# The last three steps of two attentions in another order

## The chip, the cores and the metric

The kernel runs on one core of a Trainium2 chip. The metric is the device time of one execution in microseconds; lower is better. The engines are TensorE (PE: matmuls and transposes; PEld: its weight loads), VectorE (DVE), ScalarE (ACT), GpSimd (POOL) and the queues that issue transfers (SP among them).

## The reference, cut to what matters

A block in four stages over 16 batches of 100 tokens with 512 channels, all float32: a gated cross-attention with 16 heads, a mixture of 8 experts (top two, capacity 1024), a gated cross-attention with 8 heads, and a feed-forward stage with quantized weights. Both attentions look at the same context, 722 tokens of 384 channels per batch.

```python
def attention(x, context):                    # heads = 16 (first), 8 (second)
    q = (x @ Wq).reshape(B, Nq, heads, D).transpose(0, 2, 1, 3)
    k = (context @ Wk).reshape(B, Nkv, heads, D).transpose(0, 2, 1, 3)
    v = (context @ Wv).reshape(B, Nkv, heads, D).transpose(0, 2, 1, 3)
    attn = softmax(einsum('bhqd,bhkd->bhqk', q, k) * D**-0.5)
    return einsum('bhqk,bhkd->bqhd', attn, v).reshape(B, Nq, 512) @ Wo + bo

x = x + tanh(g_xattn[0]) * attention_0(layernorm(x), ctx)   # with biases bq, bk, bv
x = x + tanh(g_ffn[0])   * experts(layernorm(x))
x = x + tanh(g_xattn[1]) * attention_1(layernorm(x), ctx)
x = x + tanh(g_ffn[1])   * quantized_ffn(layernorm(x))
```

## The kernel before

The 1600 tokens lie as 13 tiles of 128 rows (the last has 64) in one buffer `x` on the chip through all four stages. Nothing of a stage is split off: the end of one runs into the start of the next, and the order in which PE gets its work is the order of the program's text (`manual_schedule(engines={PE})`). The order on DVE, ACT, POOL and the queues is made by the compiler's scheduler, with its own costs.

An attention runs in 64 steps, `steps = [(b, m) ...]`: batch b = 0 to 15, and within it four groups m of 128 channels. A group holds G heads, G = 4 in the first attention and 2 in the second. Step i does, in this order on PE:

- `peaks` (L399, tile `ps_mx`): transposes the running maxima `mx` of step i; DVE reduces them (L405).
- `scores(i+1, 0)` (L372, `ps_s`): the next step's scores for five of the six context chunks. ACT copies them to `raw_a` (L386), DVE takes the maxima over chunks (L389, twice).
- `softmax(i)` (L413, `ps_top`): PE spreads the maxima, DVE subtracts them (L421) into `pT`, ACT takes the exponential (L427), and POOL (G = 4) or DVE (G = 2) adds up the chunks (L430, `sm`). For the last batch with m > 0 these additions are left out, and PE sums all chunks itself.
- `scores(i+1, 1)`: the sixth chunk; ACT copies it (L382), DVE takes it into `mx` (L384).
- `attend(i-1)` (L442 and L453, `ps_pv`): the weighted sum over values and the sum of weights for the step before; DVE takes the reciprocal and multiplies (L461, L462) into `tT`.

Between these PE gets units of other work: `keys` (L216) and `values` (L241) of coming batches, `queries`, the input of queries, and `project` (L468, `ps_y`), which multiplies a finished tile by Wo; DVE adds it to `x` (L475). In the first attention each projection brings `moments` (L109, L110) and, in groups, `norm_scales` (L117 to L119), `normal` (L124), `turn` (L139) and `logits` (L657) of the router. `run` gives the units out: `extra[i]` holds those with a fixed step; keys and values lie in `todo` with a first and a last step, and are taken when they are due or while the step's cost is under an even share of what remains up to step 62. `cut` gives units of up to a cost of 2000 to the place between scores and softmax (`u[0]`), the others to the end of the step (`u[1]`).

Buffers that bear on the order: `pT` has two (`p2`), the banks of `ps_m` four, `raw_a` two, `mx` one. After the first attention come the last three tiles' router work (`norm_scales(LATE, NTT)`, `turn`, `logits`, filled up with the second attention's keys), and then the experts. After the second attention come the feed-forward stage's transposes (`ps_hT`, L1058). Its weights, their loads (L1011 to L1015) and the normalization of its first four tiles (L124, L1037, L109, L1046) start while the attention's last steps run, as soon as their memory comes free; projections 11 and 12 of the second attention are tied to come after the first dequantization (L1020) on DVE. G = 4 and G = 2 differ in one more thing: with G = 4 the softmax comes before the second scores and the sum, with G = 2 after them.

Of the kernel before, what the change touches and what calls it, by code (L numbers as in the profile page):

```python
# [17 lines left out]
B, T, C = 16, 100, 512  # L18
# [5 lines left out]
KC = C // P  # L24
# [39 lines left out]
def tiles_for(b):  # L64

    return [i for i in range(NTT) if (i * P + rows_of(i) - 1) // T == b]
# [76 lines left out]
class Attention:  # L143
# [352 lines left out]
    def run(self, done=(), after_project=None, more=()):  # L496

        steps = [(b, m) for b in range(B) for m in range(KC)]  # L500
        last_tile = lambda g: ((g + 1) * GT - 1) // P
        extra = {i: [] for i in range(-1, len(steps) + 40)}
        for at, *unit in more:
            extra[at].append(tuple(unit))
        for g in range(1, B // GB):
            at = 4 * KC * (g - 1)
            for n, i in enumerate(range(last_tile(g - 1) + 1, last_tile(g) + 1)):
                extra[at + 3 + n].append((self.query_input, i))
            for m in range(KC):
                extra[at + 7 + 2 * m].append((self.queries, g, m))  # L510
        for b in range(B):
            for i in tiles_for(b):

                at = (b + 1) * KC + (1 if b != B - 2 else KC - 1)
                extra[at].append((self.project, i))
                for later, *unit in after_project(i) if after_project else ():
                    extra[at + later].append(tuple(unit))
        todo = [u for b in range(1, B) for u in self.keys_and_values(b) if u not in done]

        def do(units):  # L520
            for f, *a in units:
                f(*a)

        def first(unit):

            f, b, n = unit[:3]
            return 4 * (b - 1) + n - 1 if f == self.keys else 4 * (b - 1) if b > 1 else -1

        def last(unit):

            f, b, n = unit[:3]
            return 4 * b + n - 2 if f == self.keys else 4 * b

        end = len(steps) - 2
        for i in range(-1, len(steps)):
            b, m = steps[max(i, 0)]
            if i >= 0 and m == 2 and b + 2 < B and b + 2 not in self.cxs:
                self.load_ctx(b + 2)

            whole = sum(map(self.cost, todo + sum((extra[j] for j in range(i, end)), [])))  # L540
            share = whole / max(1, end - i)
            units = list(extra[i])
            spent = sum(map(self.cost, units))
            for unit in sorted((u for u in todo if first(u) <= i), key=last):
                if last(unit) <= i or spent + self.cost(unit) / 2 <= share:
                    units.append(unit)
                    todo.remove(unit)
                    spent += self.cost(unit)

            units.sort(key=lambda u: u[0] in (self.keys, self.values) and first(u) == i)  # L550
            nxt = steps[i + 1] if i + 1 < len(steps) else None
            u = self.cut(units, 2000)
            if i >= 0:
                self.peaks(b, m)
            if nxt:
                self.scores(*nxt, 0)
            if self.G == 4:
                do(u[0])
                if i >= 0:
                    self.softmax(b, m)  # L560
            if nxt:
                self.scores(*nxt, 1)
            if i > 0:
                self.attend(*steps[i - 1])
            if self.G == 2:
                do(u[0])
                if i >= 0:
                    self.softmax(b, m)
            do(u[1])
        self.attend(*steps[-1])  # L570
        for i in range(len(steps), len(steps) + 40):
            do(extra[i])
# [1045 lines left out]
```

## Time and profile before

| what | us |
|---|---|
| median of 3 runs | 2733.43 (2732.81 to 2734.15) |
| the profiled execution: its time, its span | 2731.8, 2730.1 |
| PE busy, share of the span | 2682.5, 98% |
| first attention, to its last projection's end | 0 to 894 |
| experts | 894 to about 1590 |
| second attention, to its first closing projection | to 2354.5 |
| feed-forward stage | to 2730 |
| DVE busy in 853.6 to 886.7 and in 2324.2 to 2354.6 | 22.3 of 33.1, 20.7 of 30.4 |
| PE busy in the same two stretches | 25.2 of 33.1, 22.0 of 30.4 |

A line of a timeline gives the start, the duration, the engine, the line of the kernel, the operation, what it writes and reads, how many instructions were merged, and in brackets how long the engine stood idle before it and whose end released it. PEclk is the clock granted to TensorE, 1.00 at full speed. Matmul ends are modelled; the distance from one start to the next is the safer measure.

### The profile page before, as it was taken

What the parts mean: (1) busy time and instruction counts of PE and PEld (TensorE: products, weight loads), DVE (VectorE), ACT (ScalarE), POOL (GpSimd) and SP (SyncE); (2) the same over time, 40 slices, a digit from 0 to 9 for tenths busy, and PEclk for the clock granted to TensorE, in tenths of its full rate; (3) what the DMA queues carried; (4) which work ended last, traced back from release to release, by engine and by line L of the source; (5) the groups of instructions that cost most, each with busy time, mean ns of one, the idle gap of its engine ahead of it and who ended that gap; (6) DMA issues with size and microseconds to landing.
All of it is one profiled execution on the core that took longest, in us unless ns stands there. A gap on an engine that the chain in (4) does not pass through costs nothing. (4 is left out here: it accounts for less than half of the span.)

```text
span 2730.1 us, 45777 instructions
## 1 busy us (share of the span) xinstructions
PE 2682.5 (98%) x19716; PEld 1740.7 (64%) x19716; DVE 1201.2 (44%) x2010; ACT 859.0 (31%) x1194; POOL 499.3 (18%) x497
## 2 busy tenths in 40 slices
PE   8999999999998999999999999999999999899999
PEld 5666666666565688888888766666666566445554
DVE  4666676666667301010101077666565555611100
ACT  2545554545454100000000046333333333311110
POOL 2534444444442000000000042000000000301000
PEclk9999999999999899999999999999999999999999
DMA  5001000010001499989899432000000010610000
GB/s 167 18 18 34 18 29 22 18 45 18 18 29 57 169 360 348 320 313 321 310 318 319 166 91 63 21 22 29 17 23 27 17 34 1 185 62 16 12 12 10
DMA packets 129190, 278.33 MB, mean 102 GB/s; under 512 B 5825, under 2 KB 5841, under 8 KB 128465
## 3 DMA queue, kind: packets, MB, share of 16 engines
q1 hardware_dynamic: 117888, 246.80, 26.2%
q0 software_dynamic: 5968, 19.17, 2.1%
q10 hardware_dynamic: 5120, 9.31, 0.9%
q8 instruction: 160, 2.62, 0.4%
q14 instruction: 54, 0.43, 0.0%
HBM read 260.31 MB, written 14.94 MB: 101 GB/s over the span
## 5 line engine op out<-in xcount | busy, mean ns | idle before, releaser
L241 PE MATMUL ps_v<-wv_a,ctx_a 128*128 128x512 f32 (+1 forms) x1152 | 520.2, 599 | 1.0 <-DVE pT L421 0.5
L216 PE MATMUL ps_k<-ctx_a,wk_a 128*128 128x361 f32 x1488 | 485.5, 473 | 3.2 <-DVE pT L421 2.1
L874 PE MATMUL ps_h<-xT,w 128*128 128x128 f32 x3712 | 422.1, 276 | 4.0 <-DVEq L1503 4.0
L874 PEld LDWEIGHTS ps_h<-xT,w 128*128 128x128 f32 x3712 | 419.5, 193 | 4.7 <-issue 4.7
L216 PEld LDWEIGHTS ps_k<-ctx_a,wk_a 128*128 128x128 f32 x1488 | 272.6, 190 | 164.0 <-issue 18.3
L241 PEld LDWEIGHTS ps_v<-wv_a,ctx_a 128*128 128x128 f32 (+1 forms) x1152 | 204.8, 184 | 243.1 <-issue 229.9
L427 ACT ACTIVATE pT<-pT 128x1200 f32<-128x1200 f32 (+1 forms) x256 | 243.2, 953 | 258.2 <-DVE pT L421 248.0
L421 DVE TENSOR_TENSOR pT<-raw_a,ps_top 128x400 f32<-128x400 f32 (+4 forms) x384 | 279.0, 771 | 11.2 <-PE ps_top L413 11.0
L430 POOL TENSOR_TENSOR sm<-pT,sm 128x400 f32<-128x400 f32 x244 | 252.5, 1035 | 38.4 <-ACT pT L427 21.7
L389 DVE TENSOR_REDUCE raw_a<-raw_a 128x400 f32<-128x1200 f32 (+1 forms) x128 | 152.1, 1188 | 218.0 <-ACT raw_a L386 217.9
L386 ACT COPY raw_a<-ps_s 128x2000 f32<-128x2000 f32 (+1 forms) x128 | 180.3, 1408 | 154.1 <-PE ps_s L372 153.7
L372 PE MATMUL ps_s<-qT_a,kT_a 32*128 32x100 f32 (+3 forms) x4608 | 214.2, 277 | 3.4 <-ACT raw_a L386 1.2
L885 DVE TENSOR_TENSOR midT<-silu,ps_h 128x512 f32<-128x512 f32 x58 | 39.9, 688 | 390.4 <-PE ps_h L874 390.4
L894 PE MATMUL ps_o<-w,midT 128*128 128x512 f32 x464 | 203.9, 592 | 0.0
L372 PEld LDWEIGHTS ps_s<-qT_a,kT_a 32*128 32x128 f32 (+3 forms) x4608 | 180.1, 180 | 35.8 <-issue 22.7
L1100 PE MATMUL ps_z<-ffn_w,y_ffn 128*128 128x512 f32 (+1 forms) x416 | 190.8, 594 | 0.0
L248 ACT COPY v_a<-ps_v 128x512 f32<-128x512 f32 x192 | 111.3, 581 | 248.3 <-PE ps_v L241 248.3
L1082 PE MATMUL ps_y<-hT,ffn_w 128*128 128x384 f32 (+2 forms) x512 | 183.6, 503 | 0.0
L442 PE MATMUL ps_pv<-pT,v_a 128*32 128x100 f32 (+3 forms) x4608 | 163.2, 254 | 7.3 <-ACT pT L427 7.3
L442 PEld LDWEIGHTS ps_pv<-pT,v_a 128*32 128x32 f32 (+3 forms) x4608 | 135.5, 120 | 22.6 <-ACT pT L427 8.7
L1082 PEld LDWEIGHTS ps_y<-hT,ffn_w 128*128 128x128 f32 x512 | 95.1, 190 | 84.6 <-issue 50.3
L894 PEld LDWEIGHTS ps_o<-w,midT 128*128 128x128 f32 x464 | 85.9, 190 | 97.1 <-issue 97.1
(169 smaller groups left out, 2211.3 us busy)
## 6 DMA issues: line engine op xcount, KB each, us to landing
w<-in_L_ffn_w SPq DMA_DIRECT2D x116, 1024.0 KB
w<-in_L_ffn_wo SPq DMA_DIRECT2D x29, 2048.0 KB
ctx_a<-in_ctxT SPq DMA_DIRECT2D x30, 1083.0 KB
q<-in_L_ffn_fc_q SPq DMA_DIRECT2D x8, 1024.0 KB
ffn_w<-in_L_ffn_fc_scales SPq DMA_DIRECT2D x8, 1024.0 KB
rows<-ot ACTq DMA_DIRECT2D x29, 256.0 KB
xn_d<-xn_moe POOLq DMA_DIRECT2D x11, 256.0 KB, 2.3
ctx_a<-in_ctxT SPq DMA_DIRECT2D x6, 361.0 KB
```

Source lines behind the costliest of these rows:

```text
L216: nc.tensor.matmul(ps, self.wk[:, k, m * P : (m + 1) * P], self.cxs[b][:, k, c * SH : (c + 1) * SH], start=(k == 0), stop=(k == KK - 1),)
L241: nc.tensor.matmul(ps[:n], self.cxs[b][:, k, c * P : c * P + n], self.wv[:, k, :], start=(k == 0), stop=(k == KK - 1),)
L372: nc.tensor.matmul(ps[:r, j, n * T : (n + 1) * T], self.kT[b, m][j * D : (j + 1) * D, c * P : c * P + r], self.qT[g][j * D : (j + 1) * D, ...
L386: nc.scalar.copy(st[:, :, :NS1, :].rearrange("p g c t -> p g (c t)"), ps[:, :, : NS1 * T])
L421: nc.vector.tensor_tensor(t[:, part, :, c:z, :], st[:, :, at : at + z - c, :], bcast(ps.unsqueeze(2), P, G, z - c, T), ALU.subtract,)
L427: nc.scalar.activation(t[:, part], t[:, part], AF.Exp)
L430: adds.tensor_tensor(sm, t[:, part, :, n, :], sm if part or n > 1 else t[:, 0, :, 0, :], ALU.add)
L442: nc.tensor.matmul(ps[j * D : (j + 1) * D, 0, :], self.v[b][:n, c, m * P + j * D : m * P + (j + 1) * D], t[:n, c // 3, j, c % 3, :], start ...
L874: nc.tensor.matmul(ph[:, f, :], w[:, n, k, f * P : (f + 1) * P], self.xT[j][:, k, :], start=(k == 0), stop=(k == KC - 1),)
L894: nc.tensor.matmul(po, self.midT[j, f // 4][:, f % 4, :], w[:, f, :], start=(f == 0), stop=(f == KF - 1),)
L1082: nc.tensor.matmul(ps[:, :nt], w1[f // nf][:, k, f % nf * P : (f % nf + 1) * P], hT[g][:, k, :nt], start=(k == 0), stop=(k == KC - 1),)
L1100: nc.tensor.matmul(z[j][:n], y[:, j * P : j * P + n], w2[f // nf][:, f % nf, :], start=(f == 0), stop=(f == NF - 1),)
```

## The change

Three things change in `run`, for both attentions. The weighted sum of step 60 is issued in step 62 (ahead of softmax 62), that of step 61 in step 63, and that of step 62 after softmax 63; the sum of step 63 stays last. With G = 4 the sum of step 61 comes after softmax 63, with G = 2 ahead of it. The values of the last batch have their last step at 61 in place of 60. Projections of the last batch's tiles, 11 and 12, get step 67 in place of 65; in the first attention this puts them behind `turn` and `logits` of tile 10, in the second nothing lies in between. In the second attention, which has no `after_project`, projection 9 goes from step 53 to step 62. The shares of the units follow from that: in the second attention they get smaller in all steps up to 56.

```diff
-                at = (b + 1) * KC + (1 if b != B - 2 else KC - 1)
+                at = (b + 1) * KC + (1 if b < B - 2 else KC - 1)
+                if b == B - 4 and after_project is None:
+                    at = len(steps) - 2
                 extra[at].append((self.project, i))
...
-            return 4 * b + n - 2 if f == self.keys else 4 * b
+            return 4 * b + n - 2 if f == self.keys else 4 * b + (b == B - 1)

         end = len(steps) - 2
+        late = len(steps) - 2
...
             if self.G == 4:
                 do(u[0])
+                if i == late:
+                    self.attend(*steps[i - 2])
                 if i >= 0:
                     self.softmax(b, m)
             if nxt:
                 self.scores(*nxt, 1)
-            if i > 0:
+            if 0 < i < late - 1:
                 self.attend(*steps[i - 1])
+            elif i > late:
+                self.attend(*steps[i - 2])
             if self.G == 2:
                 do(u[0])
+                if i == late:
+                    self.attend(*steps[i - 2])
                 if i >= 0:
                     self.softmax(b, m)
+            if i > late:
+                self.attend(*steps[i - 1])
             do(u[1])
         self.attend(*steps[-1])
```

## The prediction

> **What bounds the kernel now.** I read the page's first lines, the waits of the matrix engine (PE), and the timelines and one-microsecond windows at the ends of the two attentions (A0, A1). The page: PE is busy throughout, so a change of order can only win PE's gaps and slow-clock stretches.
>
> ```profile
> PE 2682.5 (98%) x19716; PEld 1740.7 (64%) x19716; DVE 1201.2 (44%) x2010; ACT 859.0 (31%) x1194; POOL 499.3 (18%) x497
> PE 39%; DVE 1%; DMA 1%; ACT 0%; issue 0%; POOL 0%; DVEq 0%; ACTq 0%; POOLq 0%
> ```
>
> The timeline of A0's steps 62 and 63 (start, duration, engine, line; in brackets PE's idle time and its releaser):
>
> ```profile
> 863.69 0.65 PE L399 MATMUL ps_mx<-ident,mx 128*100 128x128 f32 x4 [2.13 <-DVE mx L384]
> 867.64 0.64 PE L372 MATMUL ps_s<-qT_a,kT_a 32*82 32x100 f32 x8 [1.15 <-ACT raw_a L386]
> 870.21 2.23 PE L453 MATMUL ps_pv<-pT,ones 128*32 128x100 f32 x48
> 873.77 0.64 PE L399 MATMUL ps_mx<-ident,mx 128*100 128x128 f32 x4 [1.33 <-DVE mx L384]
> 874.25 3.60 PE L468 MATMUL ps_y<-wo_a,tT_a 128*128 128x512 f32 x8
> 877.69 0.51 PE L413 MATMUL ps_top<-ident,extremes 100*128 100x100 f32 x4
> 878.56 2.77 DVE L421 TENSOR_TENSOR pT<-raw_a,ps_top 128x1200 f32<-128x1200 f32 x3
> 879.18 1.21 PE L453 MATMUL ps_pv<-pT,ones 128*32 128x100 f32 x48
> 886.18 0.66 PE L139 MATMUL ps_tr<-ident,xn_moe 128*128 128x128 f32 x4 [1.80 <-POOL xn_moe L124]
> ```
>
> The maxima (mx) bring PE to a stand. L453 costs 2.23 us at 870 and 1.21 at 879 for the same work: the granted clock was 0.50 from about 865.4 to 872.2. A1 has the same end, worse, because the last stage's preparation (L1037, L109) stands on VectorE (DVE) too:
>
> ```profile
> 2329.55 3.98 POOL L124 TENSOR_SCALAR xn_ffn<-x,rstd,shift 128x512 f32<-128x512 f32 x4 [312.98 <-PE ps_k L216]
> 2338.02 0.64 PE L399 MATMUL ps_mx<-ident,mx 128*100 128x128 f32 x2 [3.78 <-DVE mx L384]
> 2339.59 2.27 PE L442 MATMUL ps_pv<-pT,v_a 128*64 128x100 f32 x24 [0.92 <-ACT pT L427]
> 2351.02 2.27 PE L442 MATMUL ps_pv<-pT,v_a 128*64 128x100 f32 x24 [3.43 <-ACT pT L427]
> 2354.57 1.98 PE L468 MATMUL ps_y<-wo_a,tT_a 128*128 128x512 f32 x4
> ```
>
> **The change in A1.** "Sum n" is the weighted sum of step n (attend: L442, then L453). No instruction is added or removed on any engine; the planner's arithmetic, done by hand, gives the new order. Units: a projection is 8 matmuls 0.428 us apart, 3.43 us; a values unit 6 of them, 2.57; a keys unit 1.9 (x18 took 5.65). Projection 9 leaves step 53 for 62; two values units leave step 60 for 61; the last keys unit moves from 61 to 60. Steps 53 to 56 only regroup, in stretches where PE has no gap. So the transposes of step 61 start 3.43 + 5.13 - 1.9 = 6.66 us earlier, at S = 2317.6 instead of 2324.22.
>
> From S, PE has: step 61, maxima and scores 1.78, two values 5.13, ps_top 0.3: S+7.2. Step 62, 1.78, projection 9, the sum of step 60 (1.36), ps_top 0.3: S+14.1. DVE's chain to mx(62) needs 5.5 us before and is covered. mx(63): before, it came 6.3 us after its scores (2331.71 to 2338.02) among the same L1037s; PE is there 5.1 us after, so wait 1.2. Step 63: ps_mx 0.33, sum 61 (2.2), projection 10, ps_top 0.3: S+21.6. Before, the last sum began 3.77 us after ps_top(63) began (2347.25 to 2351.02, with a table load of 1.28 in it); now sum 62 (2.2) lies in between, wait 1.25. With the last sum 2.2 PE reaches the first closing projection at S+27.2 = 2344.8, before 2354.57: **9.8 us earlier**. All idle stretches are short, so the half clock of 2336.9 to 2343.7 and 2350.7 to 2353.6 goes. Bounds: 12.2 without the two waits; 5 if both double and a dequantization (L1020, 2.28 us) is put before one of them, since projection 9's L475 (0.75) and all L109s now share a shorter stretch of DVE.
>
> Queues: SP's first ffn load waits for the last keys (2329.47 before), now S; the second kind waits for the last scores, S+9; all landed by 2343.8 before, so they land earlier too. POOL's xn_ffn waits for buffers of the last values, S+7.2 = 2324.8; its chain took 24.0 us to 2353.57, so now 2348.8, and PE wants it after both closing projections at 2352. Hidden by 3 us; without that cover each microsecond of delay counts whole. s1's second load hangs on the last sum as before and moves with it.
>
> **The change in A0.** One values unit goes from step 60 to 61, so step 61 begins at 851.02 (853.59). PE: transposes and scores 1.83, values 2.57, ps_top and late scores 0.78, two keys 3.9: 860.1. mx(62) came 6.2 us after ACT's copy ended (857.43 to 863.63); the copy now ends at 854.9, mx at 861.1: idle 1.0. Step 62: 1.9, sum 60 (1.36), ps_top, late scores: done at 865.4, as the copy allows at 865.0. Then PE has nothing: sum 61 has gone to step 63, where it stood in this gap. DVE needed 7.2 us from ps_top(62) to mx(63); from 864.9, less the 0.2 it waited, 871.9. That is 1.9 earlier than 873.77, but after 6.5 us of idle PE. Projection 10 then starts at half clock. Half clock lasted 4.0, 4.1 and 2.9 us after work resumed (868.21, 2339.59, 2351.02), a loss of 1.4 to 2.0: 1.8 here. ps_top(63): 877.69 - 1.9 + 1.8 = 877.6.
>
> The new wait: pT has two buffers, and at 16 heads softmax(63) now comes before sum 61, which still reads the third-last one. L421 is held on DVE until both halves of sum 61 are through (878.13 to 880.39 for the equal sum 62, 2.26 and a step): 2.3 us. Behind it queue the normalizations and, on ACT, the exponentials; PE does sums 61 and 62 meanwhile. Last sum ends at 886.6 (884.37). The transposes of tile 10 still wait 1.8: 888.4.
>
> Projections 11 and 12 now follow logits 10, and covered it before. The copy of the transposes (886.87 to 887.56) keeps PE 0.95, the logits take 0.91: projections end 4.1 later, 897.9. The routing's next transposes came 4.64 us after them (893.78 to 898.42), filled by logits and keys; now keys alone, so 0.7 is idle, and they stand at 902.35 for 898.42: **3.9 us later**.
>
> SP's loads for A1 hang on A0's last keys as before (861.59, now 860) and are wanted at 894.69: hidden by 20 us (landed by 874 before). POOL's adds belong to steps up to 60, and all are done by 853.3.
>
> Then the clock. The window 862.0 to 865.4 (the on and off points lie 3.4 apart) had 1.7 us idle and small matmuls, and was followed by 0.50; 882.4 to 885.9 had 1.67 and was not. Around tile 10 there will now be 1.8 + 0.95 idle within 3.4, so I take a second lowering, 3.4 us at half: 1.7. A0 loses **5.6 us**; bounds 0 (mx(63) three microseconds sooner if DVE takes both reductions first, no second lowering) to 8 (recovery a window later each time). The Trainium skill, "TensorE: Matmul & The Clock Gate" (Part 1, HAM oscillation), says that the clock falls after a whole idle window of 3.4 us; by it the second lowering fails and A0 loses 3.9. The trace speaks against it at 863.69, where 2.13 us of idle were enough.
>
> Sum: -9.8 + 5.6 = -4.2 against the profiled execution's 2731.8 (span 2730.1), 1.6 below the median of 2733.43. On the median: **2729.2**. Under 0.2% (5.5 us) a measurement of this kernel can't be told from no change; this is 0.15%.
>
> **Rivals.**
> 1. The clock falls only once in A0, because each of the two short stops stays below what the gate answers to. For: 882 to 886. Against: 863. -9.8 + 3.9 = -5.9: 2727.5. (The Trainium skill's rule above would give the same.)
> 2. DVE takes both reductions ahead of the subtractions in A0, as it did at 789 to 792; mx(63) is there at 869, three sooner, with less idle. -9: 2724.5.
> 3. A1's gap is filled only in part: DVE, with 20.7 busy of 30.4 us at 2324 to 2354, becomes the bound, gain 6: 2733.
> 4. Slower: the planner of DVE's order puts the ffn's L1037s (1.57 beside POOL), L1020 and the subtractions ahead of mx(63) and of softmax(63) in A1, PE stops there twice and runs at half clock, and the gain is gone; A0's 5.6 stays: 2739. It decides once those items cost A1 more than 9.7 us; L1037 4 x 1.57 and L1020 2.28 give 8.6. Against: PE now has more cover there.
>
> **How the numbers follow.** Forecast 0.36 (its own range 2726 to 2732), rival 1 0.22, rival 2 0.14, rival 3 0.16, rival 4 0.12. Faster by over 0.2% is below 2728: all of 2, most of 1, a quarter of the forecast, 0.40; slower is rival 4 and a little, 0.13; the rest 0.47. Predicted 2729.0. The range leaves out the far ends of 2 and 4: 2723.5 to 2736.5.
>
> **What would show it.** A1: L399 of step 63 with under 2 us idle, clock 1.00 up to the first closing projection, which starts near 2350 (2344.8 and A0's 5.6). A0: 6 us idle before the last L399, projection 10 over 4.5 us, L421 released by PE's L453, logits 10 ahead of the closing projections with a wait for DVE L140. Wrong, if L421 isn't held, if DVE's new order moves mx(63) by 3 us, or if the last stage's start doesn't follow PE.

## The result and the profile after

| | us |
|---|---|
| median after, 19 runs | 2728.20 (2726.53 to 2731.09) |
| median before, 19 runs beside it | 2732.81 (2729.05 to 2736.98) |
| ratio, with its 95% interval | 0.9986 (0.9980 to 0.9992) |
| the profiled execution after: its time, its span | 2728.79, 2727.1 |

The kernel is 4.6 us, 0.14%, faster by the medians. The interval leaves out 1, but the step is smaller than the 0.2% named above as what can be told from no change: with 19 runs on each side the interval is 0.12% wide, so that bound was too cautious. The forecast was 2729.0.

The first line of the page after, the engines' busy times:

```profile
PE 2682.2 (98%) x19716; PEld 1739.5 (64%) x19716; DVE 1201.4 (44%) x2010; ACT 860.3 (32%) x1194; POOL 500.2 (18%) x497
```

The counts of instructions are the same on every engine, and the busy times agree within 1.3 us. (ACT's count is the same by a coincidence that the experiments show: two table loads more in A0, two fewer in A1.)

The timeline of the end of the first attention (A0) after: start, duration, engine, line, operation; in brackets the idle time before it and its releaser. Lines of the kernel behind `run` have numbers 13 higher than before: the logits' L657 is now L670.

```profile
860.16 0.64 PE L399 MATMUL ps_mx<-ident,mx 128*100 128x128 f32 x4 [0.93 <-DVE mx L384]
870.49 1.09 PE L399 MATMUL ps_mx<-ident,mx 128*100 128x128 f32 x4 [5.97 <-DVE mx L384]
871.21 1.28 ACT L117 ACT_TABLE_LOAD   x1
871.38 5.17 PE L468 MATMUL ps_y<-wo_a,tT_a 128*128 128x512 f32 x8
879.16 2.78 DVE L421 TENSOR_TENSOR pT<-raw_a,ps_top 128x1200 f32<-128x1200 f32 x3 [0.88 <-PE ps_pv L453]
880.64 1.28 ACT L427 ACT_TABLE_LOAD   x1 [2.03 <-DVE pT L421]
883.19 0.72 PE L442 MATMUL ps_pv<-pT,v_a 128*32 128x100 f32 x24 [2.04 <-ACT pT L427]
884.87 2.24 PE L453 MATMUL ps_pv<-pT,ones 128*32 128x100 f32 x48
888.95 1.06 PE L670 MATMUL ps_logits<-wg_sb,xnT_moe 128*128 128x8 f32 x8 [0.78 <-DVE xnT_moe L140]
900.79 1.22 PE L139 MATMUL ps_tr<-ident,xn_moe 128*128 128x128 f32 x8
```

PE stands for 5.97 us ahead of the last maxima, then does projection 10 in 5.17 us (3.60 before). L421, the softmax of step 63, is held by L453, the sum that still reads its buffer. The logits of tile 10 wait 0.78 us for the copy L140. Half clock (a granted clock of 0.50) comes a second time, at L453 at 884.87.

The end of the second attention (A1) after, in the same view (L1037 and L1046 of before are now L1050 and L1059):

```profile
2330.61 0.75 DVE L1050 SCALAR_TENSOR_TENSOR x<-xn_ffn,tgf,x 128x512 f32<-128x512 f32 x1 [0.51 <-POOL xn_ffn L124]
2331.87 1.75 DVE L1050 SCALAR_TENSOR_TENSOR x<-xn_ffn,tgf,x 128x512 f32<-128x512 f32 x1 [0.51 <-POOL xn_ffn L124]
2334.30 0.68 DVE L109 BATCH_NORM_STATS2 st<-xn_ffn 128x6 f32<-128x512 f32 x1
2336.31 1.11 DVE L384 TENSOR_TENSOR mx<-mx,raw_a 128x200 f32<-128x200 f32 x1
2337.56 0.40 PE L399 MATMUL ps_mx<-ident,mx 128*100 128x128 f32 x2 [3.42 <-DVE mx L384]
2339.56 2.22 PE L453 MATMUL ps_pv<-pT,ones 128*64 128x100 f32 x24
2349.27 1.33 PE L442 MATMUL ps_pv<-pT,v_a 128*64 128x100 f32 x24 [1.21 <-ACT pT L427]
2351.56 7.28 PE L468 MATMUL ps_y<-wo_a,tT_a 128*128 128x512 f32 x16
```

The wait for the last maxima is still 3.42 us and the half clock behind it is still there (L453 2.22). The wait ahead of the last sum has shrunk from 3.43 to 1.21. The last stage follows PE: its first transposes start 7.21 us after the closing projections begin, before and after.

To compare executions that are already some us apart, the table takes stretches from start to start on PE. A0 is from the last-but-two maxima (L399 of step 61) to the late tiles' transposes (L139); 2.57 is added where a values unit still stands ahead of step 61, so that the same work is counted. A1 is from L399 of step 52 to L399 of step 61, and from there to the first closing projection (L468).

| kernel | A0 | A1 to step 61 | A1 from step 61 |
|---|---|---|---|
| before | 44.83 + 2.57 = 47.40 | 107.83 | 30.35 |
| after | 50.72 | 99.73 | 31.77 |
| after less before | +3.3 | -8.1 | +1.4 |

By these two executions A0 loses 3.3 us and A1 gains 6.7; their times differ by 3.0. How far such a stretch repeats for the same code is shown by the table of all kernels at the end of the experiments.

### The profile page after: what moved, and what is told of

It reads as the page before. It is cut to its first block, busy times and chain, and to the rows that moved or that the text cites. A ratio compares the mean times of both kernels' runs of the same rounds, so it can differ in the third digit from the quotient of the medians.

```text
span 2727.1 us, 45782 instructions
## 1 busy us (share of the span) xinstructions
PE 2682.2 (98%) x19716; PEld 1739.5 (64%) x19716; DVE 1201.4 (44%) x2010; ACT 860.3 (32%) x1194; POOL 500.2 (18%) x497
## 5 line engine op out<-in xcount | busy, mean ns | idle before, releaser
L421 DVE TENSOR_TENSOR pT<-raw_a,ps_top 128x400 f32<-128x400 f32 (+4 forms) x384 | 278.7, 770 | 11.5 <-PE ps_top L413 10.4
L389 DVE TENSOR_REDUCE raw_a<-raw_a 128x400 f32<-128x1200 f32 (+1 forms) x128 | 151.9, 1187 | 218.8 <-ACT raw_a L386 218.6
L389 DVE TENSOR_REDUCE mx<-raw_a 128x400 f32<-128x1200 f32 (+1 forms) x128 | 146.7, 1146 | 0.5
```

Of the source, the lines that this page charges most:

```text
L389: nc.vector.tensor_reduce(to, st[:, :, c : c + 3, :].rearrange("p g c t -> p g t c"), AX.X, ALU.max)
L421: nc.vector.tensor_tensor(t[:, part, :, c:z, :], st[:, :, at : at + z - c, :], bcast(ps.unsqueeze(2), P, G, z - c, T), ALU.subtract,)
```

## The experiments

Edits are relative to the kernel after unless said otherwise. Kernels timed together share their runs of the kernel before: a median of 2732.81 for e1 to e4, 2733.78 for e5, e6, e9 and e10, and 2732.05 for e11 and e12 (the names are those of the table at the end). A difference between kernels of two such groups is taken between their differences to the kernel before. "The change in A1 only" is called the base below.

**Each attention alone.** In the first kernel (e1) only the second attention has the change, in the second (e2) only the first.

```diff
+                if self.G != 2:            # e1; G != 4 in e2
+                    at = (b + 1) * KC + (1 if b != B - 2 else KC - 1)
...
-            return 4 * b + n - 2 if f == self.keys else 4 * b + (b == B - 1)
+            return 4 * b + n - 2 if f == self.keys else 4 * b + (b == B - 1 and self.G == 2)
...
-        late = len(steps) - 2
+        late = len(steps) - 2 if self.G == 2 else len(steps) + 2
```

> Only the second attention is changed. By the forecast's step for A1: 9.8 us earlier than before (ratio 0.9964). By the two traces, in which A1 comes 6.7 us nearer between step 50 and the first closing projection: 6.7 earlier (0.9975). The rival, that the first attention costs nothing and all of the measured 4.6 is made here: 4.6 earlier (0.9983).

> Only the first attention is changed. By the forecast: 5.6 us slower than before (1.0020), 3.9 if the clock is lowered only once. By the two traces: 3.3 slower (1.0012). The rival: no difference (1.0000). In the trace: some 6 us of idle PE ahead of the last L399, projection 10 partly at half clock, L421 of step 63 released by PE's L453.

A1 alone: 2723.93, ratio 0.9969 (0.9957 to 0.9981), so 8.9 us faster by medians and 5.2 to 11.8 by the interval. A0 alone: 2736.05, 1.0012 (1.0003 to 1.0021), 3.2 us slower, and 0.8 to 5.7 by the interval. The two add up to -0.19%, the whole change has -0.14%: there are two effects of opposite sign, and a second attention that gains no more than the whole change does, 4.6, is outside its interval. The traces show the places of before and after again. With A0 alone the last maxima of A0 come at 870.52 after 5.97 us of idle time, as in the kernel after. The last maxima of the base:

```profile
2330.45 0.64 PE L399 MATMUL ps_mx<-ident,mx 128*100 128x128 f32 x2 [3.40 <-DVE mx L384]
```

**Which part of the change costs A0 its time.** Three kernels take one part each. The first two (e3, e4) start from A0 alone; the third (e9) from the base.

```diff
                 # e3: projections 11 and 12 at step 65 again
-                at = (b + 1) * KC + (1 if b < B - 2 else KC - 1)
+                at = (b + 1) * KC + (1 if b != B - 2 else KC - 1)
```

```diff
                 # e4: sum 61 in the gap, at the end of step 62
-            elif i > late:
+            elif i == late and self.G == 4:
+                self.attend(*steps[i - 1])
+            elif i > late and self.G == 2:
                 self.attend(*steps[i - 2])
```

```diff
                 # e9: of the change in A0, the values alone
-            return 4 * b + n - 2 if f == self.keys else 4 * b + (b == B - 1 and self.G == 2)
+            return 4 * b + n - 2 if f == self.keys else 4 * b + (b == B - 1)
```

> Only the first attention is changed, and its projections 11 and 12 stay at step 65, ahead of logits 10. By the forecast's step (a wait of 0.95 for the copy and 0.7 us that the keys no longer fill): 1.7 us less than with the first attention's whole change. By the changed kernel's trace, which shows the wait of 0.8 ahead of the logits and no gap behind: 0.8 less. The rival, that the projections' place is free: no difference.

> Only the first attention is changed, and the sum of step 61 is issued at the end of step 62, in the gap ahead of the last maxima, in place of after softmax 63. By the forecast (the pT buffer is free when softmax 63 comes, and the gap is filled by 2.3 us or more): 2.3 us less than with the first attention's whole change, 3 to 4 if less idle time also shortens the half clock. The rival, that the exponential's table load and the last maxima set the end and the buffer wait is hidden: at most 1 less.

> The second attention is changed in full; in the first only the last values unit goes to step 61, with sums and projections as before. By the forecast's step for values: PE has 10.4 us of work in step 61 for a chain of 10.1, so the 2.1 us of idle ahead of L399 of step 62 goes and nothing else changes: 2.1 us less than with the second attention's change alone (about 11 less than before). The rival, that the wait only moves to the next maxima: no difference.

With the projections back: 2734.99, 1.0008 (0.9999 to 1.0017), 1.1 us less than A0 alone by medians. The trace agrees: the stretch is 49.76 in place of 50.72, and the logits, which follow the projections again, have no wait ahead of them. The intervals overlap, and only one trace has the projections back (50.72 was measured in two executions), so this 1 us is likely, not certain.

With sum 61 in the gap: 2733.32, 1.0006 (0.9997 to 1.0015), 2.7 us less by medians, 1.6 by the ratios; the stretch is 49.35, so 1.4 by the trace. These intervals overlap too. Its timeline:

```profile
869.47 1.09 PE L399 MATMUL ps_mx<-ident,mx 128*100 128x128 f32 x4 [3.79 <-DVE mx L384]
870.35 4.71 PE L468 MATMUL ps_y<-wo_a,tT_a 128*128 128x512 f32 x8
875.77 2.77 DVE L421 TENSOR_TENSOR pT<-raw_a,ps_top 128x1200 f32<-128x1200 f32 x3
883.38 0.66 PE L139 MATMUL ps_tr<-ident,xn_moe 128*128 128x128 f32 x4 [1.80 <-POOL xn_moe L124]
884.83 1.06 PE L674 MATMUL ps_logits<-wg_sb,xnT_moe 128*128 128x8 f32 x8 [0.78 <-DVE xnT_moe L140]
885.74 8.95 PE L468 MATMUL ps_y<-wo_a,tT_a 128*128 128x512 f32 x16
```

The gap shrinks by 2.18 us, a whole sum, and L421 is no longer held. But the 1.80 and 0.78 us of idle time around tile 10 are now close together, and the clock falls right behind them: the 16 matmuls of projections 11 and 12 take 8.95 us, in place of 7.26 after. So both costs named in the forecast for the sum's move, the longer gap and the hold of L421, are there; and the second fall of the clock at tile 10 that it named comes in this kernel and not in the kernel after.

The values alone, with the base in A1: 2722.34, 0.9958 (0.9944 to 0.9971), 2.6 us faster than the base by medians, with overlapping intervals. The stretch of A0 is 44.45, 2.95 less than before; it is 44.46 and 44.49 in the two later kernels with the same A0, and 47.40 to 50.00 in the five executions whose A0 is that of before. Two lines say why, and what remains:

```profile
860.23 0.60 PE L399 MATMUL ps_mx<-ident,mx 128*100 128x128 f32 x4
864.14 0.56 PE L372 MATMUL ps_s<-qT_a,kT_a 32*82 32x100 f32 x8 [1.51 <-ACT raw_a L386]
```

The 2.13 us ahead of L399 of step 62 are gone altogether, since the sum of step 60 is still there as cover beside the values. In A0, then, the values are worth some 3 us, and the later sums and projections cost some 6 (50.72 less 44.45; by medians the kernel after is 6.8 slower than this one, and their intervals lie apart).

**What holds the last maxima in A1.** DVE's timeline after has four updates of the feed-forward stage (L1050) and its moments ahead of the last L384. In this kernel (e5), made from the base, those of the first group of tiles wait on DVE until that L384 has been issued; nothing is taken away.

```diff
-            nc.vector.tensor_tensor(mx, mx, st[:, :, NS, :], ALU.max)
+            self.net.last_max = nc.vector.tensor_tensor(mx, mx, st[:, :, NS, :], ALU.max)
...
-                nc.vector.scalar_tensor_tensor(
+                ins = nc.vector.scalar_tensor_tensor(
...
+                if i in FG[0]:
+                    after(ins, net.last_max)
-                net.moments(i, xn[i])
+                ins = net.moments(i, xn[i])
+                if i in FG[0]:
+                    after(ins, net.last_max)
```

> Only the second attention is changed, and on DVE the ffn's updates of x and moments for its first four tiles stand behind the last maxima (an order, no wait for another engine). If these instructions are what held mx(63) for 3.4 us and so lowered the clock: L399 of step 63 waits under 0.5 us, no half clock up to the closing projections, and 3.4 + 1.7 = 5 us less than with the second attention's change alone (ratio about 0.995 to before). If the chain copy, two reductions, maxima itself takes that long, or the ffn's first tiles come late in place of it: within 1 us of it.

2719.82, 0.9945 (0.9932 to 0.9959): 14.0 us faster than before, 5 more than the base. Its timeline:

```profile
2328.40 0.37 DVE L384 TENSOR_TENSOR mx<-mx,raw_a 128x200 f32<-128x200 f32 x1
2330.76 0.38 PE L399 MATMUL ps_mx<-ident,mx 128*100 128x128 f32 x2
2339.83 1.43 PE L442 MATMUL ps_pv<-pT,v_a 128*64 128x100 f32 x24 [0.35 <-ACT pT L427]
```

The maxima are ready 2.0 us before PE comes to them (2328.77 and 2330.76); PE has no idle time there, no half clock follows, and 0.35 us are all that is left of the wait ahead of the last sum. So the 3.4 us and the half clock behind them came from what stood on DVE ahead of that L384, not from a lack of cover on PE. Part of it is contention and not the number of instructions: in the kernel after, the last update (L1050, 1.75) and the last L384 (1.11) ran beside POOL's additions, and took 0.75 and 0.37 where POOL was at other work or idle, 1.7 us in all. The new order moves POOL's additions away as well, since they wait for the updates, so the runs don't separate the two.

**Is projection 9's move needed?** In the base it goes back to step 53 (e6).

```diff
-                if b == B - 4 and after_project is None:
+                if False:
                     at = len(steps) - 2
```

> Only the second attention is changed, and projection 9 stays in step 53. By the forecast projection 9 fills 3.4 us of the wait for mx(63): without it PE stands that much longer, 3 us slower than the second attention's change alone. The rival, that its L475 and its place only shift the wait: no difference, or faster.

2730.34, 0.9987 (0.9978 to 0.9996): 5.4 us slower than the base. By stretches, 104.50 and 31.22 in place of 99.73 and 31.39. The wait for the last maxima is the longest of all:

```profile
2338.15 0.67 PE L399 MATMUL ps_mx<-ident,mx 128*100 128x128 f32 x2 [5.74 <-DVE mx L384]
```

With projection 9 in step 62 its 3.43 us lie where PE otherwise stands or runs slowly, since the stretch from step 61 is as long with it as without. The rest of the 4.77 by which step 61 comes sooner is mostly an idle time of 1.1 in step 54, which is back in this kernel; its cause is shown in the section on the prediction.

**Are the later sums needed?** The values and projection 9 already bring cover into the last steps. Two kernels therefore leave them there, but put the sums closer to where they were: 60 and 61 in step 62, 62 ahead of softmax 63 (the sum of step 60 can't go back to step 61, since the last values that it reads come at the end of that step). One (e11) starts from the base, the other (e12) from the best kernel (e10), which has the values alone in A0 and the order on DVE above in A1.

```diff
-            elif i > late:
-                self.attend(*steps[i - 2])
+            elif i == late:
+                self.attend(*steps[i - 2])
+                self.attend(*steps[i - 1])
+            elif i > late:
+                self.attend(*steps[i - 1])
             if self.G == 2:
                 do(u[0])
-                if i == late:
-                    self.attend(*steps[i - 2])
                 if i >= 0:
                     self.softmax(b, m)
-            if i > late:
-                self.attend(*steps[i - 1])
```

> Only the second attention is changed; its values units, keys unit and projection 9 move as in the change, and of the sums only that of step 60 (whose values now come in step 61) is issued in step 62, together with that of step 61; the sum of step 62 stays ahead of softmax 63, as before. If the later sums are part of the gain, filling PE behind the last maxima: slower than the second attention's whole change, by 1 to 3 us. If mx(63) is set by DVE alone: sum 61 (2.2 us) goes back into PE's wait ahead of it, the wait of 3.4 falls to 1.2 or so, and the last maxima are followed by less work at half clock, so 1 to 3 us faster.

> The two together: the second attention changed, the ffn's DVE work behind the last maxima, in the first only the values unit. If both act where they should: 2 + 5 us less than the second attention's change alone, some 16 us less than before (0.994). If the two stops hide behind each other: no better than the better of the two.

> As e10 (values later in both attentions, projection 9 later, the ffn's DVE work behind the last maxima), with the sums of the second attention as in the run above. In e10 PE has no wait over 0.4 us left in the second attention's tail, so the place of the sums should count for nothing there: within 1.5 us of e10 (0.9933). If the later sums are what keeps PE covered behind the last maxima: 2 us or more slower.

The best kernel: 2716.02 (2714.33 to 2717.55), 0.9933 (0.9919 to 0.9946), 17.8 us faster than before and some 13 faster than the kernel after. With the sums one step behind: 2734.80, 1.0009 (1.0000 to 1.0018) from the base, and 2728.53, 0.9987 (0.9978 to 0.9996) from the best kernel, so 11.6 and 14.2 us slower by medians; by the traces, 8.5 and 9.6 to the first closing projection and 10.2 and 9.7 to the end. The profiled execution of the second was 2.7 us faster than its median, and the rest of that difference is not explained. Both losses are larger than was expected. The sums are also not all that differs on PE: in both traces eight transposes of the last stage (1.04 us of work in the first) stand between softmax 63 and the last sum. The timeline of the one from the base:

```profile
2337.62 1.52 DVE L421 TENSOR_TENSOR pT<-raw_a,ps_top 128x600 f32<-128x600 f32 x3
2340.81 2.27 PE L442 MATMUL ps_pv<-pT,v_a 128*64 128x100 f32 x24 [6.73 <-ACT pT L427]
```

The spread maxima of step 62 (L413, 2333.07 and 0.34 long) were on their bank at 2333.4. DVE came to them at 2337.62, behind four moments (L109), a reciprocal and the addition of a projection; sum 62 is next in PE's order and wants the exponentials of these, and projection 10, whose input is older, stands behind it. From the best kernel, with the order on DVE, the same wait is 4.10 us:

```profile
2333.38 2.27 PE L442 MATMUL ps_pv<-pT,v_a 128*64 128x100 f32 x24 [4.10 <-ACT pT L427]
```

So in A1, by these timelines, the later sums are not only cover for the last wait: they let PE go on with the sums of an older step while DVE and ACT make the next softmax.

All kernels, in the order of their times, with the ratio to the kernel before; the stretches are those of the profiled execution, A0 with 2.57 added where a values unit stands ahead of step 61:

| kernel | median us | ratio (95%) | A0 | A1 to 61 | from 61 |
|---|---|---|---|---|---|
| A0: values alone; A1: change and order on DVE (e10) | 2716.02 | 0.9933 (0.9919 to 0.9946) | 44.46 | 99.74 | 25.65 |
| A1 and order on DVE (e5) | 2719.82 | 0.9945 (0.9932 to 0.9959) | 47.41 | 99.73 | 25.65 |
| A0: values alone; A1: change (e9) | 2722.34 | 0.9958 (0.9944 to 0.9971) | 44.45 | 99.73 | 32.36 |
| A1 only, the base (e1) | 2723.93 | 0.9969 (0.9957 to 0.9981) | 47.91 | 99.73 | 31.39 |
| after | 2728.20 | 0.9986 (0.9980 to 0.9992) | 50.72 | 99.73 | 31.77 |
| best, sums one behind (e12) | 2728.53 | 0.9987 (0.9978 to 0.9996) | 44.49 | 99.73 | 35.25 |
| base, projection 9 back (e6) | 2730.34 | 0.9987 (0.9978 to 0.9996) | 50.00 | 104.50 | 31.22 |
| A0 only, sum 61 in the gap (e4) | 2733.32 | 1.0006 (0.9997 to 1.0015) | 49.35 | 107.84 | 30.31 |
| base, sums one behind (e11) | 2734.80 | 1.0009 (1.0000 to 1.0018) | 48.12 | 99.73 | 39.85 |
| A0 only, projections back (e3) | 2734.99 | 1.0008 (0.9999 to 1.0017) | 49.76 | 107.84 | 31.42 |
| A0 only (e2) | 2736.05 | 1.0012 (1.0003 to 1.0021) | 50.72 | 107.83 | 31.56 |

The same code differs between executions. In the last column it is up to 1.3 us (30.31 in e4 and 31.56 in A0 only; 31.39 and 32.36 in e1 and e9). In the column of A0 it is 2.6 for the code of before (47.40 before, 47.91, 47.41, 50.00 and 48.12 in e1, e5, e6 and e11), but nothing for the whole change (50.72 twice) and 0.04 for the values alone. A difference below these is not read from one trace.

## Why the prediction was right, and where its steps were not

The time came within 1 us of the forecast, by the mechanism that was forecast: a gain in A1, less a smaller loss in A0. Both terms were too large, by about as much, so part of the hit is luck, two errors that cancel: -9.8 + 5.6 was forecast, and the traces have -6.7 + 3.3. Over all pairs of traces with the same code A1's gain is 6.1 to 8.3 and A0's loss 0.7 to 3.3, so neither reaches the forecast. The times of the two attentions alone, -8.9 (5.2 to 11.8) and +3.2 (0.8 to 5.7), show the two signs, but their intervals hold the forecast's sizes as well. A1's gain is near rival 3's 6; with that and the forecast's 5.6 for A0 the time would have been 2733.

A1, step by step:

- "S 6.66 us earlier": 8.1. The missing 1.4 is in "Steps 53 to 56 only regroup, in stretches where PE has no gap", which was wrong. The timeline before has a gap there: scores wait 1.09 us for a keys' copy (L230, at 2242.24), and on ACT a table load for the last stage's square root (L117) stands ahead of that copy. The root comes as soon as projection 9 has been added. With projection 9 in step 62 this load and the gap are gone, and with it back in step 53 (e6) both are there again (2241.54, and 1.1 us of idle time at 2243.53):

```profile
2240.74 1.28 ACT L117 ACT_TABLE_LOAD   x1 [0.49 <-DVE mean L110]
2242.73 1.09 PE L372 MATMUL ps_s<-qT_a,kT_a 64*128 64x100 f32 x16 [1.09 <-ACT kT_a L230]
```

- PE's order from S to ps_top(62): 13.97 us to its start, where S+14.1 was given for its end. Right, and the maxima of step 62 were covered.
- "mx(63) wait 1.2": 3.42. This is the step that failed. It took the 6.3 us that the maxima had needed after their scores before, and carried them over; they now needed 8.7 (2328.84 to 2337.56), because the scheduler put three of the four updates, two moments and an average between the scores and the last L384, and POOL's additions beside them. The order on DVE (e5) takes the whole wait away, so the cause is shown. It is a part of rival 4's mechanism, the updates without the dequantization, at some 4 us (2.2 of wait and 1.9 of slower clock) of the 9.7 that rival 4 needed, and DVE's bound in rival 3: the forecast had put 0.28 on the two.
- "so the half clock goes": it stayed, as a result of the same wait (2338.8 to 2342.3). Ps_mx to ps_top(63) took 8.2 us where 6.3 were worked out.
- "wait 1.25" ahead of the last sum: 1.21. Right.
- POOL's xn_ffn and the last stage's start hidden behind PE: right, 7.21 us before and after.

From S to the closing projection 31.77 us stand against 27.2: 2.2 of the difference from the wait, 1.9 from the clock and a short wait for L475, 0.4 from the rest.

A0, step by step:

- Idle 1.0 ahead of mx(62): 0.93. Idle 6.5 ahead of mx(63): 5.97. Projection 10 slower by 1.8: by 1.6. Logits' wait 0.95: 0.78. Right.
- L421 held 2.3 us by sum 61: ps_top(63) was through at about 876.9 and L421 began at 879.16. Right; and with sum 61 in the gap (e4) the hold is gone.
- "The transposes of tile 10 still wait 1.8": they don't. ACT loaded the table of the square root (L117) at 871.21, 0.7 us behind the end of PE's gap, and took tile 10's root at 878.31, ahead of the last exponentials; POOL then normalized the tile during the last sum. The price is a load of the exponential's table at 880.64 (1.28 us) and one more of the root's at 884.25 (with the change in A0 alone ACT has 1196 instructions, 1194 before; that no instruction is added was wrong here), and so a last sum that waits 2.04 and 0.37 in place of 0.90 and 0.60.
- "A second clock lowering 1.7 around tile 10": it came ahead of tile 10, in the last sum, and cost about 1.5 (L453 2.24 for 1.21, L139 1.12 for 0.66). With it and without tile 10's wait, the closing projections ended 4.2 us later than before (897.05, and 0.95 for the earlier step 61, less 893.78), where 4.1 + 1.7 were forecast: 1.6 of the 2.3 by which 5.6 was too much.
- "0.7 is idle" ahead of the late transposes: none. They start 3.74 us after the keys begin, in place of the 4.45 that were worked out. That is the other 0.7.

Rival 1, in which the clock falls once, is refuted by L453. Of rival 2 only the order came. DVE did take both reductions of step 63 (L389, at 864.22 and 865.75) ahead of the subtractions, as it said, but the maxima were not there three microseconds sooner, because the last L384 was put behind all three subtractions:

```profile
867.18 2.77 DVE L421 TENSOR_TENSOR pT<-raw_a,ps_top 128x1200 f32<-128x1200 f32 x3
869.87 0.57 DVE L384 TENSOR_TENSOR mx<-mx,raw_a 128x400 f32<-128x400 f32 x1
```

Its input from ACT (L382) was there at 865.13. Ahead of the subtractions it could have ended 2.7 us sooner, an estimate from these rows, and shortened PE's stop of 5.97 by as much. That is the order on DVE again, as in A1; no run tries it in A0.

The Trainium skill, "TensorE: Matmul & The Clock Gate" (Part 1, HAM oscillation), has the clock fall after a whole idle window of 3.4 us. The runs show less to be enough. In A0 2.04 and 0.37 us of idle, with half a values sum between them, were followed by half clock, and so were 1.80 and 0.78 with four transposes between them in the kernel with sum 61 in the gap. In A1 the stop of 3.42 us is as long as that, but the 3.41 us just ahead of the half clock (2335.43 to 2338.84) hold 1.10 us of work on PE. The measurement decides here: the second lowering that the forecast took came, though not at tile 10.

## What to carry to other kernels

Work moved into a gap only helps as far as the engine that ends the gap keeps its order: look at what the scheduler puts ahead of the awaited instruction, since here a few of DVE's instructions put behind one L384 were worth 5 us, as much as the whole change (4.6). A sum that is put off gives cover where it lands and takes it from where it stood, and it holds its buffer longer: with three steps' weights in two buffers the next softmax waits, and what is queued behind it on DVE and ACT waits too. Two attentions of the same code are two cases, and a move that pays in one is to be measured alone in the other.

## What the runs showed of the hardware that was not expected

The clock falls on less than a long stop. In the kernel with the values alone, one stop of 1.51 us (862.6 to 864.1) and small matmuls around it were followed by half clock. One-microsecond windows show the edges; after the window come its length, the busy time and number of instructions of PE, PEld, DVE, ACT and POOL, then the granted clock, the DMA share and the GB/s:

```profile
864.00:865.00 1.00, 0.86 (x20) 0.66 (x24) 1.00 (x3) 0.85 (x2) 0.00 (x0) 0.64 0.88 238
867.00:868.00 1.00, 1.00 (x39) 1.00 (x32) 1.00 (x1) 1.00 (x1) 0.00 (x0) 0.65 0.90 332
```

Worked out from the clocks of such windows, half clock lasted 3.41 us in each of four places: 864.28 to 867.70 here, 884.76 to 888.18 and 2338.84 to 2342.26 after, 886.23 to 889.65 with sum 61 in the gap. In other places it lasted a whole number of times as long: 6.83 at 867.70 after and at 865.61 before, 13.65 at 862.33 with projection 9 back. All its edges in one trace lie whole multiples of 3.41 us apart. The Trainium skill, "TensorE: Matmul & The Clock Gate" (Part 1, The HAM clock gate), gives about 3.4 us of steady work for the way back to full speed, and the four places agree.

So the 3.41 us ahead of an edge are the place to look. In the kernel after 0.24, 1.20 and 1.10 us of work on PE (from 864.28, 881.35 and 2335.43) were followed by half clock, and 2.38 (from 2345.67, with the stop of 1.21 us at 2348) were not. In between it goes both ways. The first of these lines is of the kernel with the values alone and was followed by half clock; the second is of the kernel before, holds most of the stop of 1.80 us ahead of tile 10, and was not:

```profile
860.87:864.28 3.41, 1.90 (x48) 1.61 (x52) 2.24 (x4) 2.13 (x3) 0.00 (x0) 1.00 0.84 236
882.68:886.09 3.41, 1.70 (x72) 1.47 (x72) 1.36 (x6) 1.48 (x2) 0.73 (x1) 1.00 0.00 0
```

In the kernel before, the 3.41 us ahead of the first fall in A0 (862.20 to 865.61) hold 1.92 us of work, more than the 1.70 that weren't followed by half clock; the prediction read more idle time there, from a window placed 0.2 us off. So neither the length of one stop nor PE's busy time in the window alone decides; what else counts stays open. Where the edges fall differs from execution to execution: the same A0 had 6.83, 6.83, 6.83, 13.65 and 3.41 us of half clock in its last steps in the five executions named under the table, and the one with 13.65 has the longest stretch, 50.00.

An instruction on DVE with two inputs was slow beside one of the same kind on POOL. The last L384 took 1.11 us in the kernel after, beside POOL's additions (L1059, busy from 2331.81 to 2337.19), and 0.37 in e5, where POOL stood idle at that time; the update L1050 took 0.75 beside POOL's L124, which has one tensor input, and 1.75 as L1059 began. The Trainium skill, "GPSIMD Engine Reference" (Specifications), says that the two engines share their interfaces to the on-chip memory and get in each other's way where DVE has two inputs from it; the trace agrees.

What was not tried: a third buffer for `pT` in A0, which should end the hold of L421 with the sums left late, and in A0 the last L384 ahead of the subtractions.
